# A second queue for the weights of a graph network, and another order for the head of its last layer

## The chip, the cores and the metric

The kernel runs on one core of a Trainium2 chip. The metric is the time of one execution in device microseconds (us), as the median of several runs. A profile of one execution is read beside it. Engines are named as the profile names them: PE (TensorE, with PEld for its weight loads), DVE (VectorE), ACT (ScalarE), POOL (GpSimd) and SP (SyncE). ACT, POOL and SP each issue DMAs on a queue; the letter q behind an engine's name (ACTq) marks that in the trace.

## The reference

There are 16 graphs of 1024 nodes with 128 channels. `x` is [16, 1024, 128], `adj` is [16, 1024, 1024] of zeros and ones. Two layers, each added to its input and normalised over the channels. Cut to what matters:

```python
# layer 0: four steps of a gated graph convolution
h = x
for i in range(4):
    hw = jnp.einsum('bnc,cd->bnd', h, weight[i])
    m = jnp.einsum('bjn,bjd->bnd', adj, hw)
    h = _gru_cell(m, h, w_ih[i], w_hh[i], b_ih[i], b_hh[i])
x = layernorm(x + h * nodemask)
# layer 1: neighbours thinned row by row, then three SAGE steps
adj_d = dilate(adj)                       # each row's removals touch later rows
def sage(x, Wr, Wx, b):
    agg = einsum('bij,bjd->bid', adj_d, x) / clip(sum(adj_d, -1), 1)
    out = agg @ Wr + x @ Wx + b
    return out / max(norm(out), 1e-12) * nodemask
h1 = bn(relu(sage(x, Wr1, Wx1, b1)), g1, be1)   # bn: over all graphs and nodes
h2 = bn(relu(sage(h1, Wr2, Wx2, b2)), g2, be2)
h3 = bn(relu(sage(h2, Wr3, Wx3, b3)), g3, be3)
x = layernorm(x + (concat([h1, h2, h3]) @ Wl + bl) * nodemask)
```

## The kernel before

**Stages.** `Gated` computes layer 0 and, woven into it, `FixPoint` thins the neighbours of layer 1: the GRU's matrix products fill PE, the thinning fills what DVE and ACT have left. Two streams of graphs alternate, so that one's products stand beside the other's element work. `Sage` then makes three passes over all graphs (`first`, `second`, `third`); a batch norm needs the statistics of all 16 graphs before the next pass can begin. `head_weights` makes the last batch norm and what follows from it, and `last`, the head, computes the output.

**Order of the work.** In all these stages the order of the instructions on each engine is the order in which the code emits them (`manual_schedule`), except that some are moved up within their engine where nothing holds them. Each engine runs its instructions one after the other; an instruction that waits holds all that stand behind it on its engine, and DMA issues are such instructions too. Each queue serves its own DMAs.

**Start.** `run` of `Gated` loads x of the first graph (L1021, POOL), then `load_weights` (L947 to L963) issues 14 DMAs on ACT's queue: for each of the four steps 64 KB of `weight`, 192 KB of `w_ih` and 192 KB of `w_hh` (L955, L959; tiles `h_w`, `h_ms`, `h_r`, `h_z`, `h_zh`), then the two biases (L963). POOL's queue brings eight 512 KB tiles of the first graph's adjacency (L1016, `h_a`), as fp32r for the products, and four 256 KB tiles `f_a` for the thinning. `prepare` turns every weight on PE (L974, L977), folds `weight` into `w_ih` (L981) and turns the biases (L986). `begin` (L1049) and the main loop follow: L1092 are the products of the adjacency with the high part (`h_hi`) and the low part (`h_lo`) of h, L1104 the gates.

In a gate, DVE adds (L1116, L1118) and `rest` (L1030) computes the low part for the next step, from a PSUM bank that PE needs again. POOL does the last three operations of the GRU cell (L1123 to L1125).

**h_test.** The kernel for the usual input holds only if the adjacency is zeros and ones. `load_test(n)` (L991 to L994) brings 128 rows of it on SP's queue, `check(n)` (L996) calls `look` (L2028), one DVE pass over the 128x1024 tile. `load_test(0)` is SP's second DMA, its check stands among DVE's operations of the first layer. Any other value sets a flag, and a general version follows, which the input here does not need.

**Third pass.** `third` (L1875 to L1927) goes through 32 units, half graphs, in stages: products of unit i, normalised rows of unit i - 2 (L1429), transposes of unit i - 3 on PE (L1450), ACT's copy of unit i - 4 into `r3` (L1916), statistics of unit i - 5 (L1909). For each unit DVE adds the other product to `acc` (L1927), the sum that the head needs. Its PSUM pool has eight banks: two each of `q_oa` and `s_tr`, two of the double tile `q_ob`.

**Head weights.** `batch_norm(2)` (L1328 to L1333) aggregates the statistics and makes scale and shift, `scaled` (L1336) makes `wr2`, the scaled part of Wl. The shifts of the three batch norms go through Wl into a 48x128 matrix `v`: DVE copies each shift to 48 columns (L1376), PE multiplies (L1377), and a fourth pair (L1379, L1380) brings the bias. `parts` (L1343 to L1350) splits v into three bf16 parts, the rows `r48`.

**Head.** `last` (L1930 to L2001) goes over the graphs. `row(b)` (L1942) takes from r48 what belongs to graph b, on POOL. `head(b)` does two halves: four fp32 products of `r3` with `wr2` (L1953), for the second half a product of `acc` with the unit matrix (L1957), which adds acc in PSUM, and four bf16 products of the mask with the row (L1961). For the first half DVE adds acc instead (L1964). DVE's bn_stats (L1968) and bn_aggr (L1970) make mean and variance of each node, ACT the root (L1972). `norm(b)` on the graph before: DVE makes scale and shift (L1977, L1978), and POOL (L1984, one of eight), ACT (L1988, seven of eight) or, for the last graph, DVE write the normalised result, which a DMA brings out.

## Time and profile before

| | before |
|---|---|
| median of 3 runs | 2176.11 us |
| lowest and highest | 2175.39, 2177.13 us |
| the profiled execution | 2176.16 us |
| its span in the profile | 2174.3 us |
| mean granted clock of PE | 0.988 |
| bytes moved by DMA | 406.16 MB |

The span is the time from the first to the last recorded work; what lies around it belongs to the execution's time too. "Busy" is time with an instruction in work; register, branch and semaphore instructions do not count. In a timeline each line gives start, duration, engine, line of the code, operation, output<-inputs, and how many instructions of a kind stand behind one another (xcount, with their joint duration). In brackets stand the engine's idle time just before and what ended it. Start times overlap a little, because instructions are pipelined. The granted clock tells what share of TensorE's full speed the throttle allowed.

### The profile page before, as it was taken

The numbers are of one execution on the slowest core, as the hardware profiler recorded it, in microseconds if no ns is written. First come the engines' busy times: TensorE is split into PE (matmuls) and PEld (weight loads), VectorE is DVE, ScalarE is ACT, GpSimd is POOL, SyncE is SP. The second block draws the span as 40 slices with busy tenths as digits, with TensorE's granted clock in tenths as the row PEclk, the third lists the DMA queues.
The fourth block names the chain that finished last, engine by engine and source line by source line (L and its number), as shares of the span: only waits on it lengthen the run. The fifth ranks groups of instructions, "written<-read, shape, count | busy, mean of one in ns | idle before, by whom it ended". The sixth has DMA issues, their size and how long they took to land. (4 is left out here: it accounts for less than half of the span.)

```text
span 2174.3 us, 33161 instructions
## 1 busy us (share of the span) xinstructions
PE 2063.3 (95%) x10217; PEld 1438.1 (66%) x10217; DVE 1831.1 (84%) x4313; ACT 1312.8 (60%) x3142; POOL 1324.3 (61%) x1346
## 2 busy tenths in 40 slices
PE   6999999999999999999999978999999889999987
PEld 3666556666556665566655656777777768887876
DVE  4898998988998889998889978888888777676888
ACT  3657557566565656656566466666666545555757
POOL 4458558567467476476575456777777545555852
PEclk9999999999999999999999989999999999999989
DMA  8348356347446276455394349888888677775515
GB/s 258 77 93 252 92 126 225 82 133 214 101 143 195 75 210 155 96 190 132 79 266 104 74 166 318 305 297 307 304 305 306 209 243 271 265 262 185 158 40 157
DMA packets 233856, 406.16 MB, mean 187 GB/s; under 512 B 79042, under 2 KB 100196, under 8 KB 233668
## 3 DMA queue, kind: packets, MB, share of 16 engines
q1 hardware_dynamic: 187844, 284.37, 40.7%
q0 software_dynamic: 41472, 117.46, 20.1%
q10 hardware_dynamic: 4352, 2.11, 0.4%
q8 instruction: 83, 1.36, 0.3%
q14 instruction: 105, 0.86, 0.1%
HBM read 313.48 MB, written 109.25 MB: 194 GB/s over the span
## 5 line engine op out<-in xcount | busy, mean ns | idle before, releaser
L1104 PE MATMUL h_g<-h_h,h_wh 128*128 128x512 f32 x768 | 396.1, 597 | 3.3 <-DVE h_r L1116 3.3
L1104 PE MATMUL h_g<-h_ms,h_wi 128*128 128x512 f32 x768 | 392.3, 592 | 0.0
L1123 POOL TENSOR_TENSOR h_zh<-h_r,h_h 128x512 f32<-128x512 f32 x126 | 174.1, 1382 | 257.9 <-ACT h_r L1119 254.7
L737 DVE TENSOR_TENSOR_SCAN f_rank<-f_a,f_first,f_pd 128x1024 f16<-128x1024 bf16 x128 | 299.4, 2345 | 4.2
L1092 PE MATMUL h_g<-h_a,h_hi 128*128 128x512 f32 x1024 | 278.6, 413 | 1.1 <-DMA h_a<-in_adj_dram 1.0
L1536 POOL CAST p_b<-p_at 128x512 uint8<-128x512 f32 x256 | 219.4, 878 | 84.3 <-DVE p_at L1528 52.3
L1104 PEld LDWEIGHTS h_g<-h_ms,h_wi 128*128 128x128 f32 x768 | 145.6, 190 | 184.2 <-issue 168.6
L1092 PE MATMUL h_g<-h_a,h_lo 128*128 128x512 f32 x1024 | 261.9, 393 | 0.4 <-DVE h_lo L1030 0.4
L1092 PEld LDWEIGHTS h_g<-h_a,h_hi 128*128 128x128 f32 x1024 | 190.1, 188 | 61.7 <-issue 21.0
L1092 PEld LDWEIGHTS h_g<-h_a,h_lo 128*128 128x128 f32 x1024 | 189.8, 188 | 39.0 <-DVE h_lo L1030 0.8
L1104 PEld LDWEIGHTS h_g<-h_h,h_wh 128*128 128x128 f32 x768 | 133.4, 190 | 100.3 <-issue 72.9
L1125 POOL TENSOR_TENSOR h_h<-h_h,h_zh 128x512 f32<-128x512 f32 x126 | 179.9, 1427 | 9.9
L1119 ACT ACTIVATE h_r<-h_r,h_bi 128x512 f32<-128x512 f32 x128 | 92.4, 722 | 150.1 <-DVE h_r L1118 150.1
L1124 POOL TENSOR_TENSOR h_zh<-h_z,h_zh 128x512 f32<-128x512 f32 x126 | 162.0, 1285 | 9.9
L1095 ACT COPY h_ms<-h_g 128x512 f32<-128x512 f32 x128 | 73.8, 576 | 150.7 <-PE h_g L1092 150.7
L1403 ACT ACTIVATE s_junk<-s_o 128x128 bf16<-128x128 f32 x256 | 76.1, 298 | 141.6 <-DVE s_o L1396 141.6
L910 ACT ACTIVATE f_u<-f_rank,f_q 128x128 f16<-128x128 f16 (+7 forms) x128 | 110.6, 867 | 69.7 <-DVE f_rank L850 69.7
L2028 DVE SCALAR_TENSOR_TENSOR p_junk<-p_a 128x1024 bf16<-128x1024 f32 x96 | 125.8, 1311 | 0.0
L1803 PE MATMUL q_ob<-s_wxp,q_xt 128*128 128x256 f32 x512 | 123.5, 385 | 0.0
L778 POOL TENSOR_SCALAR_AFFINE_SELECT f_both<-f_both 128x512 bf16<-128x512 bf16 x32 | 20.4, 639 | 164.2 <-DVE f_both L777 164.2
L1528 DVE SCALAR_TENSOR_TENSOR p_at<-p_nr,p_u 128x128 fp32r<-128x128 bf16 (+1 forms) x192 | 102.4, 543 | 20.2 <-ACT p_at L1520 14.8
L887 ACT ACTIVATE f_pd<-f_rank,f_q 128x128 f32<-128x128 f16 x128 | 59.1, 462 | 96.6 <-DVE f_q L701 93.4
(273 smaller groups left out, 4900.9 us busy)
## 6 DMA issues: line engine op xcount, KB each, us to landing
h_a<-in_adj_dram POOLq DMA_DIRECT2D x128, 512.0 KB, 9.1
p_a<-in_adj_dram SPq DMA_DIRECT2D x96, 512.0 KB
f_a<-in_adj_dram POOLq DMA_DIRECT2D x128, 256.0 KB, 6.5
e_nr<-f_nr SPq DMA_DIRECT2D x128, 256.0 KB
p_nr<-e_nr SPq DMA_DIRECT2D x32, 1024.0 KB
h_test<-in_adj_dram SPq DMA_DIRECT2D x32, 512.0 KB
s_at<-p_b SPq DMA_DIRECT2D x32, 512.0 KB
s_ag<-s_ag SPq DMA_DIRECT2D x64, 256.0 KB
```

The source lines that it names most:

```text
L737: nc.vector.tensor_tensor_scan(out, a, other[:, 0, 0:1].to_broadcast([P, N]), start, op0=ALU.add, op1=ALU.bypass)
L910: nc.scalar.activation(u[:, :n1], rank[:, g, :n1], AF.Abs, bias=q[:, 1, g:g + 1], scale=q[:, 0, g:g + 1])
L1092: nc.tensor.matmul(pm[f], part[:, j, :], st.adj[j][:, half[f]], start=(j == 0 and n == 0), stop=(j == NB - 1 and n == 1))
L1104: nc.tensor.matmul(pg, lhs, rhs, start=(i == 0), stop=(i == len(mm) - 1))
L1119: nc.scalar.activation(r, r, AF.Tanh, bias=bias(self.bi, 2))
L1123: aid.tensor_tensor(d, r, h, ALU.subtract)
L1124: aid.tensor_tensor(d, z, d, ALU.mult)
L1125: aid.tensor_tensor(h, h, d, ALU.add)
L1528: self.nc.vector.scalar_tensor_tensor(g["at"][:, j, c0:c0 + low], v[:, j, c0:c0 + low], 0.0, pu[:, :low], op0=ALU.is_lt, op1=ALU.is_lt)
L1536: self.nc.gpsimd.tensor_copy(g["b", f][:, j, :], g["at"][:, j, f * HF:(f + 1) * HF].bitcast(F32))
L1803: nc.tensor.matmul(pb[:, i], g["xt"][:, f, blk], self.wxp, start=(i % 2 == 0), stop=False)
L2028: nc.vector.scalar_tensor_tensor(junk, a, 0.0, a, op0=ALU.is_gt, op1=ALU.not_equal, accum_out=bad[:, c:c + 1])
```

## The change

- `load_weights`: w_hh's four DMAs and both biases go to SP's queue; `weight` and w_ih stay on ACT's.
- `load_test(0)` goes from SP's queue to POOL's, where it stands behind the second L1125 of the first stream's first layer. DVE's check keeps its place.
- `third` and `last` share one PSUM pool. The head's banks are those of the third pass (`head_banks`); for 8 of the 16 graphs both halves lie in one `q_ob` tile.
- `head_weights` is now within the head's schedule. It first starts the second halves of graphs 0 and 1 with the unit-matrix product (`start_half`), ahead of their other products, then two 128x512 bf16 products into a bank that nobody reads. In PE's order, the two unit products stand between the transposes of the third pass's units 29 and 30, the two idle products behind those of unit 31. After v's products graph 2's half is started too.
- The last unit's addition to `acc` stands on DVE behind the four copies for v. Those for the first two batch norms, which the old order had moved up into earlier passes, now stand with the others; their tile has two buffers as before.
- Row 0 is made by DVE; u_rb has four buffers rather than three.
- The mask products of a half come after the main products of the next half (`half`, `finish`).
- For 15 graphs mean and variance come from six POOL operations on 128x8 tiles (`moments`) in place of eight bn_aggr on DVE; the last graph keeps bn_aggr, behind all its statistics.
- `norm` goes 4 to 7, then 0 to 3, with POOL on two of eight and ACT on six. The root of a graph is emitted after the norm of the graph before.

```diff
--- before.py
+++ after.py
@@ -956,11 +956,11 @@
             for n, src in enumerate((w_ih, w_hh)):
                 t = wk.tile([C, HF], F32, name=next(names))
                 t = self.w_in[l, n] = t[:, :3 * C].rearrange("p (g c) -> p g c", g=3)
-                nc.scalar.dma_start(t, src[l].rearrange("(g p) c -> p g c", p=C))
+                (nc.scalar, nc.sync)[n].dma_start(t, src[l].rearrange("(g p) c -> p g c", p=C))
         t = wk.tile([P, NB, C], F32, name="h_x", bufs=3)
         self.b_in = [t[:L0 * 3, i, :] for i in range(2)]
         for t, src in zip(self.b_in, (b_ih, b_hh)):
-            nc.scalar.dma_start(t, src.rearrange("l (g c) -> (l g) c", c=C))
+            nc.sync.dma_start(t, src.rearrange("l (g c) -> (l g) c", c=C))
 
     def prepare(self):
         nc, ident = self.nc, self.cst["ident"]
@@ -991,7 +991,7 @@
     def load_test(self, n):
         if n < B * 2:
             self.test = self.wk.tile([P, N], F32, name="h_test", bufs=1)
-            self.nc.sync.dma_start(self.test, self.adj[n // 2, n % 2 * P:(n % 2 + 1) * P, :])
+            (self.nc.sync if n else self.nc.gpsimd).dma_start(self.test, self.adj[n // 2, n % 2 * P:(n % 2 + 1) * P, :])
 
     def check(self, n):
         junk = self.wk.tile([P, N], BF, name="h_junk", bufs=1)
@@ -1366,11 +1366,16 @@
         nc.tensor.matmul(v, self.sel01[:, l, :], self.vr, start=(l == 0), stop=True)
         self.parts(v, self.part6, self.r6[:6, :])
 
-    def head_weights(self, ps):
+    def head_weights(self):
         nc, K = self.nc, 3 * B
+        v = self.ps2.tile([P, 4, P], F32, name="s_tr")[:K, 0, :]
+        junk = self.ps2.tile([P, 4, P], F32, name="s_tr").rearrange("p a b -> p (a b)")
+        for b in range(2):
+            self.start_half(b)
+        for i in range(2):
+            nc.tensor.matmul(junk, self.cst["ident_b"], self.mask48[:, :HF], start=True, stop=True)
         self.batch_norm(2)
         self.scaled(self.wr2, self.wl[:, 2, :], 2)
-        v = ps.tile([K, C], F32, name="s_v48")
         for l in range(3):
             beta = self.small.tile([C, K], F32, name="s_beta48")
             nc.vector.tensor_copy(beta, self.ab[l][:, 1:2].to_broadcast([C, K]))
@@ -1378,10 +1383,27 @@
         beta = self.small.tile([C, K], F32, name="s_beta48")
         nc.vector.tensor_copy(beta[:10, :], self.cst["ident"][:10, 9:10].to_broadcast([10, K]))
         nc.tensor.matmul(v, beta[:10, :], self.vr, start=False, stop=True)
+        nc.vector.tensor_add(*self.late)
+        self.start_half(2)
         r48 = self.one.tile([P, C], BF, name="s_r48")
         nc.gpsimd.memset(r48, 0.0)
         self.parts(v, self.part48, r48[:K, :])
         return r48
+
+    def head_banks(self, b):
+        ps = self.ps2
+        if b % 4 in (0, 3):
+            self.banks[b] = [ps.tile([P, 4, C], F32, name="s_tr" if b % 4 else "q_oa") for f in range(2)]
+        else:
+            t = ps.tile([P, 4, 2, C], F32, name="q_ob").rearrange("p a b c -> p (a b) c")
+            self.banks[b] = [t[:, :4, :], t[:, 4:, :]]
+
+    def start_half(self, b):
+
+        acc = self.acc[:, b, 4:, :]
+        self.head_banks(b)
+        self.nc.tensor.matmul(self.banks[b][1].rearrange("p a b -> p (a b)"), self.cst["ident"],
+                              acc.rearrange("p a b -> p (a b)"), start=True, stop=False)
 
 
     def scale_rows(self, b, f, pa, pb, scalar=False):
@@ -1878,7 +1900,7 @@
         with ExitStack() as c:
             pool = lambda name, **k: c.enter_context(tc.tile_pool(name=name, **k))
...
@@ -1924,63 +1946,89 @@
                 if i < len(units):
                     g["ss", f] = self.shared_squares(g["o", f])
                     acc = self.acc[:, b, 4 * f:4 * f + 4, :]
-                    nc.vector.tensor_add(acc, pb[:, :, 1, :], acc)
-
-
-    def last(self, r48):
+                    self.late = acc, pb[:, :, 1, :], acc
+                    if i + 1 < len(units):
+                        nc.vector.tensor_add(*self.late)
+
+
+    def last(self):
         nc, tc, cst = self.nc, self.tc, self.cst
         with ExitStack() as c:
             pool = lambda name, **k: c.enter_context(tc.tile_pool(name=name, **k))
             wk = pool("u_wk", bufs=6)
-            ps = pool("u_ps", bufs=8, space=PSUM)
             c.enter_context(tc.manual_schedule(engines={ET.PE, ET.DVE, ET.Activation, ET.Pool, ET.SP}))
+            r48 = self.head_weights()
             st = {}
 
             def row(b):
                 if b < B:
-                    st["row", b] = wk.tile([P, C], BF, name="u_rb", bufs=3)
-                    nc.gpsimd.tensor_scalar(st["row", b], r48, self.graph[:, b:b + 1], None, op0=ALU.mult)
-
-            def head(b):
-                rb = st.pop(("row", b))
-                row(b + 2)
-                y = wk.tile([P, NB, C], F32, name="u_y")
-                mv = self.small.tile([P, NB, 2], F32, name="p_mv")
-                for f in range(2):
-...
+            def half(b, f):
+
+                ahead = b < 3 and f
+                if f == 0:
+                    row(b + 2)
+                    if b not in self.banks:
+                        self.head_banks(b)
+                pp, acc = self.banks[b][f], self.acc[:, b, 4 * f:4 * f + 4, :]
+                for i in range(4):
+                    nc.tensor.matmul(pp[:, i, :], self.r3[:, b, f, i * P:(i + 1) * P], self.wr2,
+                                     start=(i == 0 and not ahead), stop=False)
+                if f and not ahead:
+                    nc.tensor.matmul(pp.rearrange("p a b -> p (a b)"), cst["ident"],
+                                     acc.rearrange("p a b -> p (a b)"), start=False, stop=False)
+
+            def finish(b, f):
+                pp, acc = self.banks[b][f], self.acc[:, b, 4 * f:4 * f + 4, :]
+                for i in range(4):
+                    k = 4 * f + i
+                    nc.tensor.matmul(pp[:, i, :], self.mask48[:, k * P:(k + 1) * P], st["row", b],
+                                     start=False, stop=(i == 3))
+                if not f:
+                    st["y", b] = wk.tile([P, NB, C], F32, name="u_y")
+                    st["s6", b] = self.small.tile([P, NB, 6], F32, name="u_st")
+                    nc.vector.tensor_add(st["y", b][:, :4, :], pp, acc)
+                s6, src = st["s6", b], pp if f else st["y", b]
+                for i in range(4):
+                    nc.vector.bn_stats(s6[:, 4 * f + i, :], src[:, i, :])
+
+            def moments(b):
+                y, pp, s6 = st.pop(("y", b)), self.banks.pop(b)[1], st.pop(("s6", b))
+                st.pop(("row", b))
+                if b < B - 1:
+
+                    mv = self.small.tile([P, 4, NB], F32, name="u_mv")
+                    total, gap, spread, var = (mv[:, i, :] for i in range(4))
+                    nc.gpsimd.tensor_tensor(gap, s6[:, :, 1], s6[:, :, 4], ALU.subtract)
+                    nc.gpsimd.tensor_tensor(spread, s6[:, :, 2], s6[:, :, 5], ALU.add)
+                    nc.gpsimd.tensor_tensor(gap, gap, gap, ALU.mult)
+                    nc.gpsimd.tensor_scalar(gap, gap, C / 4.0, 0.0, op0=ALU.mult, op1=ALU.add)
+                    nc.gpsimd.tensor_tensor(var, gap, spread, ALU.add)
+                    nc.gpsimd.tensor_tensor(total, s6[:, :, 1], s6[:, :, 4], ALU.add)
+                    st[b] = y, pp, total, var, -0.5, 1.0 / C
+                else:
+                    mv = self.small.tile([P, NB, 2], F32, name="p_mv")
+                    for k in range(NB):
+                        nc.vector.bn_aggr(mv[:, k, :], s6[:, k, :])
+                    st[b] = y, pp, mv[:, :, 0], mv[:, :, 1], -1.0, 1.0
+
+            def root(b):
+                rs = st["rs", b] = self.small.tile([P, 2, NB], F32, name="u_rs")
+                nc.scalar.activation(rs[:, 0, :], st[b][3], AF.Sqrt, bias=self.eps, scale=st[b][5])
 
             def norm(b):
-                y, pp, mv, rs = st.pop(b)
+                y, pp, mean, _, share, _ = st.pop(b)
+                rs = st.pop(("rs", b))
                 nc.vector.reciprocal(rs[:, 0, :], rs[:, 0, :])
-                nc.vector.scalar_tensor_tensor(rs[:, 1, :], mv[:, :, 0], -1.0, rs[:, 0, :],
+                nc.vector.scalar_tensor_tensor(rs[:, 1, :], mean, share, rs[:, 0, :],
                                                op0=ALU.mult, op1=ALU.mult)
-                for k in range(NB):
+                for k in (4, 5, 6, 7, 0, 1, 2, 3):
                     src = pp[:, k - 4, :] if k > 3 else y[:, k, :]
                     scale, shift = rs[:, 0, k:k + 1], rs[:, 1, k:k + 1]
-                    if k == 0 or (b, k) == (B - 1, 1):
+                    if k < 2:
                         nc.gpsimd.tensor_scalar(y[:, k, :], src, scale, shift, op0=ALU.mult, op1=ALU.add)
                     elif b == B - 1 and k > 2:
                         nc.vector.tensor_scalar(y[:, k, :], src, scale, shift, op0=ALU.mult, op1=ALU.add)
@@ -1994,11 +2042,23 @@
 
             row(0)
             row(1)
-            for b in range(B + 1):
-                if b < B:
-                    head(b)
-                if b:
-                    norm(b - 1)
+            halves = [(b, f) for b in range(B) for f in range(2)]
+            for h in range(len(halves) + 1):
+                if h < len(halves):
+                    half(*halves[h])
+                if h < 1:
+                    continue
+                b, f = halves[h - 1]
+                finish(b, f)
+                if f:
+                    moments(b)
+                    if b == B - 1:
+                        root(b)
+                    if b:
+                        norm(b - 1)
+                    if b < B - 1:
+                        root(b)
+            norm(B - 1)
 
     def run(self):
         tc, nc = self.tc, self.nc
@@ -2016,10 +2076,9 @@
         with tc.tile_pool(name="s_psw", bufs=1, space=PSUM) as ps:
             self.weights(2, ps.tile([6, C], F32, name="s_v6"))
         self.r3 = self.ctx.enter_context(tc.tile_pool(name="s_r3p", bufs=1)).tile([C, B, 2, HF], F32, name="s_r3")
-        self.third()
-        with tc.tile_pool(name="s_psw", bufs=1, space=PSUM) as ps:
-            r48 = self.head_weights(ps)
-        self.last(r48)
+        with tc.tile_pool(name="t_ps2", bufs=2, space=PSUM) as self.ps2:
+            self.third()
+            self.last()
 
 
 def look(nc, junk, bad, a, b, k):
```

More of the change, by code (lines that the diff above doesn't have):

```diff
@@ L1880, in third @@
             self.wk = pool("t_wk", bufs=3)
-            self.ps2 = pool("t_ps2", bufs=2, space=PSUM)
+            self.banks = {}
             c.enter_context(tc.manual_schedule(engines={ET.PE, ET.DVE, ET.Activation, ET.Pool, ET.SP}))
@@ L1940, in row @@
                 if b < B:
-                    st["row", b] = wk.tile([P, C], BF, name="u_rb", bufs=3)
-                    nc.gpsimd.tensor_scalar(st["row", b], r48, self.graph[:, b:b + 1], None, op0=ALU.mult)
-            def head(b):
-                rb = st.pop(("row", b))
-                row(b + 2)
-                y = wk.tile([P, NB, C], F32, name="u_y")
-                mv = self.small.tile([P, NB, 2], F32, name="p_mv")
-                for f in range(2):
-                    acc = self.acc[:, b, 4 * f:4 * f + 4, :]
-                    pp = ps.tile([P, 4, C], F32, name="u_p")
-                    for i in range(4):
-                        nc.tensor.matmul(pp[:, i, :], self.r3[:, b, f, i * P:(i + 1) * P], self.wr2,
-                                         start=(i == 0), stop=False)
-                    if f:
-                        nc.tensor.matmul(pp.rearrange("p a b -> p (a b)"), cst["ident"],
-                                         acc.rearrange("p a b -> p (a b)"), start=False, stop=False)
-                    for i in range(4):
-                        k = 4 * f + i
-                        nc.tensor.matmul(pp[:, i, :], self.mask48[:, k * P:(k + 1) * P], rb,
-                                         start=False, stop=(i == 3))
-                    if not f:
-                        nc.vector.tensor_add(y[:, :4, :], pp, acc)
-                    s6 = self.small.tile([P, 4, 6], F32, name="p_st")
-                    src = pp if f else y
-                    for i in range(4):
-                        nc.vector.bn_stats(s6[:, i, :], src[:, i, :])
-                    for i in range(4):
-                        nc.vector.bn_aggr(mv[:, 4 * f + i, :], s6[:, i, :])
-                rs = self.small.tile([P, 2, NB], F32, name="u_rs")
-                nc.scalar.activation(rs[:, 0, :], mv[:, :, 1], AF.Sqrt, bias=self.eps)
-                st[b] = y, pp, mv, rs
@@ new lines, in row @@
+                    st["row", b] = wk.tile([P, C], BF, name="u_rb", bufs=4)
+                    (nc.gpsimd if b else nc.vector).tensor_scalar(st["row", b], r48, self.graph[:, b:b + 1], None,
+                                                                  op0=ALU.mult)
+            def half(b, f):
[11 more added lines that the diff above has]
+                                     acc.rearrange("p a b -> p (a b)"), start=False, stop=False)
```

## The prediction

> **What bounds the kernel now.** The summary and the slices come first: TensorE (PE) is busy for 95% of the span, every other engine for 84% or less, so the time is PE's work plus the places where PE stands still. The slices show two of those, the first and the last.

> ```profile
> span 2174.3 us, 33161 instructions
> PE 2063.3 (95%) x10217; PEld 1438.1 (66%) x10217; DVE 1831.1 (84%) x4313; ACT 1312.8 (60%) x3142; POOL 1324.3 (61%) x1346
> PE   6999999999999999999999978999999889999987
> PEclk9999999999999999999999989999999999999989
> ```

> The change touches exactly these ends, so I read the timeline of each. PE's timeline from 4 to 36 us (start, duration, line, out<-in, count, idle before and its releaser):

> ```profile
> 13.23 0.90 PE L974 MATMUL h_g<-ident,h_r 128*128 128x128 f32 x3 [5.40 <-DMA h_r<-in_L_gnn_w_ih_dram]
> 17.68 0.90 PE L974 MATMUL h_g<-ident,h_r 128*128 128x128 f32 x3 [3.55 <-DMA h_r<-in_L_gnn_w_hh_dram]
> 23.55 0.87 PE L974 MATMUL h_g<-ident,h_z 128*128 128x128 f32 x3 [4.76 <-DMA h_z<-in_L_gnn_w_ih_dram]
> 27.14 0.88 PE L974 MATMUL h_g<-ident,h_z 128*128 128x128 f32 x3 [2.72 <-DMA h_z<-in_L_gnn_w_hh_dram]
> ...
> 33.81 2.09 PE L1092 MATMUL h_g<-h_a,h_hi 128*128 128x512 f32 x8
> ```

> PE waits four times for weights; the last set starts at 28.02, and 5.8 us later the main loop begins (33.81). From there PE has no idle time (26.00 us busy in 34 to 60, 40.00 in 60 to 100): each microsecond by which the loop starts earlier is one off the time, and each stall of PE behind it is one on it.

> The DMA view of 10 to 20 us says why weights are late:

> ```profile
> q0 software_dynamic: 933, 2.75, 90.6%
> q10 hardware_dynamic: 934, 0.45, 22.3%
> ```

> One packet of q0 (POOL's, adjacency) passes for one of q10 (ACT's, weights), 93 a microsecond each, though a weight packet is a sixth as large. From 26 to 27 us, with q0 nearly empty, q10 moves 523.

> **Start: the weights' queue.** Weights' packets number 3824 in all, of which q10 had moved 1259 by 8 us; 2565 are left. With w_hh on SP's queue there would be two weight packets to one of q0. A q0 packet takes 16 x 0.906 / 93.3 = 0.155 us of an engine, a q10 packet 0.038; together 0.193, in which 0.171 passed (16 / 93.4), so a third packet makes the round 0.205 us: 78 packets a microsecond for each queue, 156 for weights.
> From 2 to 5 us q1 (mostly h_test, which leaves) took 77, 78 and 40% of the engines, 1.96 us of all of them, or 1025 weight packets at 523. If none of that is used, 2565 / 156 = 16.4 and the weights end at 24.4; if all is, 1540 / 156 = 9.9 and they end at 17.9. I take the middle, 21.1. With the 5.9 us from the last landing (27.9) to the loop, it starts at 27.0, 6.8 us earlier. The late end gives 30.3, 3.5 earlier. The early end meets another transfer: q0 loses slots (78 rather than 94 a microsecond), so its 1717 packets after 8 us are through at about 27.9; the loop needs its last tile 1.8 us after its begin, so it starts no earlier than 26.1, 7.7 earlier. Gain **6.8** (3.5 to 7.7).
> ACT issues 8 DMAs where it issued 14 (from 3.94 to 23.47 us, two of which stood 6.54 and 4.21 us); SP has nothing else to do then.

> [...]

> **Start: h_test.** SP issues it at 1.24 us; POOL would after its second L1125 of the first layer, which here ends at 58.79. POOL then idles 7.80 us, so the issue delays nothing. Behind it stands DVE's check, in its old place:

> ```profile
> 57.83 2.04 DVE L2028 SCALAR_TENSOR_TENSOR h_junk<-h_test 128x1024 bf16<-128x1024 f32 x1
> ...
> 62.89 0.49 DVE L864 TENSOR_SCALAR f_w<-f_u,f_q 128x1024 bf16<-128x1024 f16 x1 [0.68 <-ACT f_u L913]
> 63.41 0.69 DVE L866 TENSOR_TENSOR f_nr<-f_w,f_a 128x1024 bf16<-128x1024 bf16 x1
> 64.78 0.49 DVE L864 TENSOR_SCALAR f_w<-f_u,f_q 128x1024 bf16<-128x1024 f16 x1 [0.67 <-ACT f_u L913]
> ...
> 66.43 0.74 DVE L1116 SCALAR_TENSOR_TENSOR h_r<-h_g,h_bh,h_r 128x512 f32<-128x512 f32 x1
> 67.28 0.69 DVE L1118 TENSOR_TENSOR h_r<-h_g,h_r 128x512 f32<-128x512 f32 x1
> 67.89 0.68 DVE L1030 TENSOR_TENSOR h_lo<-h_g,h_hi 128x512 fp32r<-128x512 f32 x1
> ```

> Such a 512 KB load lands after 3.4 us (e_sum, when DMA is quiet) to 5.5 (the fastest h_a; h_x takes 5.1): 4.6 taken, so the check starts at 63.4, 5.6 late. The waits for ACT (0.68 + 0.67) cover 1.35; beside an idle POOL the check takes about 0.8 less (1.22 at 96.12). L1030 is then 3.4 late, and PE, whose product at 68.82 needs its bank and has 0.25 spare, stands 3.2 us (2.0 to 4.2). This moves with the loop, so it counts in full. Cost **3.2**; net of the start -3.6 (-7.7 + 2.0 = -5.7, to -3.5 + 4.2 = +0.7).

> **Head: before its first products.** PE's timeline between third pass and head:

> ```profile
> 2099.81 1.09 PE L1450 MATMUL s_tr<-ident,s_r 128*128 128x128 f32 x4 [1.25 <-DVE s_r L1429]
> 2101.57 1.09 PE L1377 MATMUL s_v<-s_wl,s_beta 128*48 128x128 f32 x4 [0.67 <-ACT s_r L1916]
> 2104.82 0.66 PE L1377 MATMUL s_v<-s_wl,s_beta 128*48 128x128 f32 x2 [2.17 <-DVE s_beta L1376]
> 2105.41 0.66 PE L1380 MATMUL s_v<-s_vr,s_beta 10*48 10x128 f32 x2
> 2106.85 0.55 PE L1953 MATMUL u_p<-s_wr,s_r 128*128 128x128 f32 x1 [0.78 <-DVE s_rest L1344]
> ```

> DVE's chain sets it: L1429, bn_stats, L1328, root, wr2 (ends 2104.41), beta, v, split, row(0) on POOL (2108.43, 0.60), masks 2109.09. In order:
> - L1927 (0.68) goes behind v: some 0.5 off the last two normalisations, 1.25 of PE's wait being for them.
> - The betas 0 and 1, copied in earlier passes until now, follow wr2 on DVE, and the tile has two buffers, so beta 2 waits for PE: four copies (0.19) and products (0.33 warm, twice that cold), two more than now, +0.7 warm, +1.0 cold; I take +0.8.
> - row(0) on DVE takes 0.34 (L1350, the nearest) less a hand-over: -0.5 of 0.60 + 0.1.
> - Three unit products of 0.86 leave the head's PE stretch for idle time ahead: -2.6. The first two stand between the transposes of units 29 and 30; 1.7 us in PE's gaps of 0.40 and 1.25 push those transposes by up to 0.6, already in DVE's slack at 2099.6 if the clock is full.
> - Clock: PE is granted 1.00 until 2099.4 and 0.50 until 2113.04. 6.2 us of products there cost 3.1 over the warm rows (1.09 against 0.63 for four transposes, 2.04 against 1.11 for L1953). Products in the gaps could keep it (-3.1) or not (0).

> These do not add in full. DVE's chain to the first masks gains 0.5 - 0.8 + 0.5 = 0.2. Behind the first masks PE is the bound, without idle time until the end: there the three unit products are missing (-2.6), and of the clock's 3.1 I count half (-1.5, between all and nothing). The transposes pushed back cost +0.5. PE's end: -0.2 - 2.6 - 1.5 + 0.5 = **-3.8** (-1 to -6).

> [...]

> **Head: steady state.** PE's period per graph is 3.20 us without idle (0.86 + 0.23 + 0.95 + 0.22 + 0.95; 2118.57 to 2121.78). DVE's is the same (0.72, 0.79, 0.32, 0.81, 0.28, 0.28); moving bn_aggr (0.60) to POOL frees DVE, not PE: 0. ACT loses one of seven (0.38), hidden too. The wait that is new: both halves of 8 graphs share one tile, so masks of half 1 wait for DVE's addition of half 0; a half behind, they have over a microsecond for its 0.7. I estimate 0.1 each: **+0.8** (0 to 2).
> POOL: row 0.60, two norms 0.88, six 128x8 operations. Their bounds are 0.106 (memset 128x16) and 0.44 (128x128); nearest is 48x3, 0.182, so 0.15 plus a gap of 0.08: 1.48 + 6 x 0.23 = 2.9, under 3.20.
> Behind PE's end: now DVE does bn_stats and aggr of half 1; then the addition, eight bn_aggr (0.6) and masks come later in order: **+1.3** (0.5 to 2). Head: -3.8 + 0.8 + 1.3 = **-1.7** (+1 to -4).

> **Sum.** Profiled run 2176.16 (span 2174.3 and 1.86 around it; the median 2176.11 is 0.05 less): 2176.16 - 3.6 - 1.7 = **2170.9**; ends 2176.16 - 5.7 - 4 = 2166.5 and 2176.16 + 0.7 + 1 = 2177.9.

> **Rivals.**
> - A: the sum, 2166.5 to 2171.7: 0.55.
> - B: weights move no faster, or h_test's wait eats it: for it speaks DMA at 9 tenths until 27 us, against it the small share (22%) of weights. Start 0, head -1.7: 2174.5. 0.18.
> - C: the clock is already low when the unit products run (2 x 1.71 us in front of two transposes), so they delay the chain by 2: start -3.6, head about 0: 2172.6. 0.12.
> - D, slower: POOL becomes the head's bound. At 0.29 us a moment operation POOL's graph takes 3.20; from there it decides. At 0.44 it takes 1.48 + 2.64 = 4.1, 0.9 more on 15 graphs, +14: 2170.9 + 14 = 2185. 0.15.

> [...]

> Measurement tells 0.2% (4.35 us) from no change. Faster than 2171.8 is A: 0.55; same (B and C): 0.30; slower (D): 0.15. Range **2166.5 to 2178**: all but D and a rest of A.

> **What would show it.** L974's last wait ends near 21 us, L1092 starts near 27; the check waits about 5.6 us for h_test and PE about 3 for L1030; granted clock 1.00 through the head; PE's period 3.20 with POOL's moments under 0.2 each; POOL as releaser of ACT's roots would be D. I am wrong if weights and adjacency end together as now, or if the head's chain waits on POOL.

## The result and the profile after

The changed kernel is faster by 0.4%: 2165.86 us (median of 5 runs, 2164.98 to 2169.4) beside 2176.7 for the kernel before (5 runs), ratio 0.9958 with a 95% interval of 0.9946 to 0.9969, so 6.7 to 11.8 us. Run once more beside other kernels it gave 0.9963 (0.9949 to 0.9976), so 8.1 us. The forecast was 2170.9, 5.3 us less than the profiled run before; the gain by the medians, 10.8, is twice that. By the ratio the time is 2167.0 beside 2176.16, near the fast end of the range (2166.5), and the median itself lies 0.6 past that end. The profiled run after took 2169.40, the slowest of its five and 6.8 less than before's 2176.16; its span is 7.0 shorter.

The page after, the lines that answer to those of before:

```profile
span 2167.3 us, 33169 instructions
PE 2065.3 (95%) x10218; PEld 1441.3 (67%) x10219; DVE 1826.0 (84%) x4194; ACT 1307.0 (60%) x3127; POOL 1345.7 (62%) x1451
PE   7999999999999999999999979999999989999987
PEclk9999999999999999999999989999999999999999
```

The shares say nothing here: the same 95%, of a shorter span. The ends have to be read one by one. PE's timeline at the start, after:

```profile
...
9.79 1.54 PE L974 MATMUL h_g<-ident,h_r 128*128 128x128 f32 x6 [2.82 <-DMA h_r<-in_L_gnn_w_ih_dram]
...
16.59 1.51 PE L974 MATMUL h_g<-ident,h_z 128*128 128x128 f32 x6 [5.05 <-DMA h_z<-in_L_gnn_w_ih_dram]
...
22.20 1.52 PE L974 MATMUL h_g<-ident,h_zh 128*128 128x128 f32 x6 [3.88 <-DMA h_zh<-in_L_gnn_w_ih_dram]
...
23.72 4.29 PE L981 MATMUL h_g<-h_wi,h_w 128*128 128x384 f32 x8
...
28.84 2.09 PE L1092 MATMUL h_g<-h_a,h_hi 128*128 128x512 f32 x8
```

The last weights are there at 22.2 rather than 28.0, the loop begins at 28.84 rather than 33.81: 4.97 earlier. Between the two lie 6.64 us, where before had 5.79; L981 alone takes 4.29 where it took 3.46. DMA's view of 10 to 20 us, and of 12 to 14 within it, after:

```profile
q0 software_dynamic: 880, 2.51, 85.2%
q10 hardware_dynamic: 806, 0.39, 15.5%
q1 hardware_dynamic: 546, 0.25, 12.7%
```

```profile
q0 software_dynamic: 163, 0.30, 79.5%
q1 hardware_dynamic: 163, 0.08, 19.5%
q10 hardware_dynamic: 164, 0.08, 13.3%
```

From 12 to 14 us all three have work and each moves 82 packets a microsecond (78 forecast). SP's share is through by 18 us, ACT's, the longer one, by 22. DVE's and PE's timelines around h_test's check, after:

```profile
57.66 1.23 DVE L2087 SCALAR_TENSOR_TENSOR h_junk<-h_test 128x1024 bf16<-128x1024 f32 x1 [4.71 <-DMA h_test<-in_adj_dram]
...
63.83 0.75 DVE L1116 SCALAR_TENSOR_TENSOR h_r<-h_g,h_bh,h_r 128x512 f32<-128x512 f32 x1
64.68 0.69 DVE L1118 TENSOR_TENSOR h_r<-h_g,h_r 128x512 f32<-128x512 f32 x1
65.29 0.68 DVE L1030 TENSOR_TENSOR h_lo<-h_g,h_hi 128x512 fp32r<-128x512 f32 x1
```

```profile
64.64 1.13 PE L1104 MATMUL h_g<-h_h,h_wh 128*128 128x512 f32 x2 [0.61 <-DVE h_r L1116]
```

DVE does wait for h_test, 4.71 us, and L1116 comes 2.37 late measured from the loop's begin. But PE loses 0.61 there. The same product of PE before, which waits for nothing:

```profile
68.82 1.02 PE L1104 MATMUL h_g<-h_h,h_wh 128*128 128x512 f32 x2
```

And the head, PE's timeline after:

```profile
2091.28 1.31 PE L1405 MATMUL q_oa<-s_acc,ident 128*128 128x512 f32 x2
2092.39 1.91 PE L1405 MATMUL q_ob<-s_acc,ident 128*128 128x512 f32 x2
2094.09 1.63 PE L1472 MATMUL s_tr<-ident,s_r 128*128 128x128 f32 x8
2095.83 0.38 PE L1376 MATMUL s_tr<-s_mask,ident_b 128*128 128x512 bf16 x1
2099.70 1.57 PE L1382 MATMUL s_tr<-s_wl,s_beta 128*48 128x128 f32 x6 [3.50 <-DVE s_beta L1381]
2101.20 0.66 PE L1385 MATMUL s_tr<-s_vr,s_beta 10*48 10x128 f32 x2
2101.78 2.08 PE L1405 MATMUL q_ob<-s_acc,ident 128*128 128x512 f32 x2
2103.65 2.85 PE L1978 MATMUL q_oa<-s_wr,s_r 128*128 128x128 f32 x16
2106.34 0.39 PE L1988 MATMUL q_oa<-u_rb,s_mask 128*128 128x128 bf16 x4
```

From v's products on PE stands still only once more until its last, for 0.18 us (2112.53, waiting for DVE's addition of a graph whose two halves share a tile), so the wait of 3.50 us ahead of them is the last one that counts. The unit product of graph 2 (2101.78) lies behind it, in the stretch that PE bounds, and at half clock (0.50 below). The granted clock by stretches (columns: window, length, busy time of PE, PEld, DVE, ACT, POOL, clock, DMA share, GB/s), after:

```profile
2091.90:2095.30 3.40, 3.40 (x9) 1.78 (x9) 2.62 (x7) 0.28 (x2) 0.00 (x0) 0.50 0.00 0
2095.30:2098.70 3.40, 0.80 (x5) 0.34 (x4) 2.47 (x4) 1.34 (x3) 0.00 (x0) 1.00 0.00 0
2098.70:2105.50 6.80, 5.80 (x19) 3.78 (x20) 4.22 (x18) 0.00 (x0) 0.93 (x2) 0.50 0.00 0
```

The clock falls at 2091.9, recovers at 2095.3, and falls again at 2098.7, late in PE's wait before v, until 2105.5: one length of 3.4 and then two. POOL's moments, after, one graph:

```profile
2149.53 0.21 POOL L2005 TENSOR_TENSOR u_mv<-u_st 128x8 f32<-128x8 f32 x1 [1.07 <-DVE u_rs L2025]
2149.70 0.20 POOL L2006 TENSOR_TENSOR u_mv<-u_st 128x8 f32<-128x8 f32 x1
2149.86 0.20 POOL L2007 TENSOR_TENSOR u_mv<-u_mv 128x8 f32<-128x8 f32 x1
2150.15 0.20 POOL L2008 TENSOR_SCALAR u_mv<-u_mv 128x8 f32<-128x8 f32 x1
...
2150.79 0.88 POOL L2032 TENSOR_SCALAR u_y<-u_y,u_rs 128x128 f32<-128x128 f32 x2
```

At most 0.21 each, 1.26 for six: POOL's graph takes 0.60 + 0.88 + 1.26 = 2.74, under PE's 3.20.

**By sections.** One execution of a kernel differs from the next by several microseconds (after's five runs take 2164.98 to 2169.4), so I cut each profile at five events: the loop's first product; the PE product that waits for L1116 at 243.16 in before; DVE's last product sum of the third pass (L1396, 2094.73 in before); PE's last product; the span's end.

| profile | loop begins | to 243.16's event | to third's last sum | to PE's end | to the end | span |
|---|---|---|---|---|---|---|
| before | 33.81 | 209.35 | 1851.57 | 66.71 | 12.86 | 2174.3 |
| after | 28.84 | 210.07 | 1850.21 | 64.46 | 13.72 | 2167.3 |
| after again (e13) | 30.00 | 210.13 | 1850.64 | 64.48 | 13.35 | 2168.6 |
| e1 start only | 28.91 | 209.95 | 1851.42 | 66.54 | 12.58 | 2169.4 |
| e2 head only | 33.88 | 208.95 | 1853.36 | 62.31 | 13.40 | 2171.9 |
| e3 test early | 29.17 | 210.05 | 1849.43 | 64.45 | 14.00 | 2167.1 |
| e4 more idle | 29.37 | 209.93 | 1850.90 | 64.15 | 13.35 | 2167.7 |
| e5 aggr on DVE | 27.02 | 210.35 | 1850.06 | 65.51 | 13.66 | 2166.6 |
| e6 none ahead | 28.65 | 210.60 | 1848.95 | 65.53 | 13.87 | 2167.6 |
| e7 beta ahead | 26.96 | 210.34 | 1849.78 | 61.68 | 14.14 | 2162.9 |
| e9 moments twice | 26.71 | 210.22 | 1849.77 | 72.47 | 14.63 | 2173.8 |
| e10 late in place | 27.82 | 210.18 | 1850.12 | 64.70 | 13.38 | 2166.2 |
| e11 early, beta | 28.07 | 210.09 | 1849.81 | 61.67 | 13.36 | 2163.0 |
| e12 as e11, idle | 31.39 | 209.14 | 1851.50 | 61.69 | 13.88 | 2167.6 |

After against before: -4.97 + 0.72 - 1.36 - 2.25 + 0.86 = -7.0. The third term lies in stages that the change leaves alone, but for two small copies that only before and e1 have there. Those 1850 us spread over 4.4 us in the table (1848.95 to 1853.36). The clock is one thing that differs in them. PE's timeline of before and then of after, at the third pass's begin:

```profile
1986.86 3.54 PE L1803 MATMUL q_ob<-s_wxp,q_xt 128*128 128x256 f32 x8
...
1991.41 1.89 PE L1803 MATMUL q_ob<-s_wxp,q_xt 128*128 128x256 f32 x8
```

```profile
1982.37 1.89 PE L1825 MATMUL q_ob<-s_wxp,q_xt 128*128 128x256 f32 x8
```

Eight products take 3.54 in one and 1.89 in the other: before was granted half clock there (0.50 from 1986.78 to 1990.19), after full (1.00). But this place does not explain the term. The whole stretch, before and then after (columns as above):

```profile
243.16:2094.73 1851.57, 1783.65 (x8947) 1254.99 (x8947) 1578.65 (x3569) 1134.46 (x2767) 1167.92 (x1159) 0.99 0.63 193
238.91:2089.12 1850.21, 1785.18 (x8947) 1257.37 (x8947) 1580.35 (x3566) 1134.59 (x2767) 1166.98 (x1160) 0.99 0.63 193
```

PE is busy 1.53 us longer after, and idle 2.89 less (65.03 rather than 67.92). By the traces' clock records half clock adds up to 27.3 us there before and to 37.6 after, so on the whole the clock was against the changed kernel. Why PE stood still less is open.

### The profile page after: what moved, and what is told of

The parts are those of the page before. It is cut to its first block, busy times and chain, and to the rows that moved or that the text cites. A ratio compares the mean times of both kernels' runs of the same rounds, so it can differ in the third digit from the quotient of the medians.

```text
span 2167.3 us, 33169 instructions
## 1 busy us (share of the span) xinstructions
PE 2065.3 (95%) x10218; PEld 1441.3 (67%) x10219; DVE 1826.0 (84%) x4194; ACT 1307.0 (60%) x3127; POOL 1345.7 (62%) x1451
## 3 DMA queue, kind: packets, MB, share of 16 engines
q8 instruction: 83, 1.36, 0.3%
q10 hardware_dynamic: 2704, 1.31, 0.2%
## 5 line engine op out<-in xcount | busy, mean ns | idle before, releaser
L1123 POOL TENSOR_TENSOR h_zh<-h_r,h_h 128x512 f32<-128x512 f32 x126 | 174.3, 1383 | 256.9 <-ACT h_r L1119 253.7
L1092 PE MATMUL h_g<-h_a,h_hi 128*128 128x512 f32 x1024 | 278.0, 413 | 0.2
L1092 PE MATMUL h_g<-h_a,h_lo 128*128 128x512 f32 x1024 | 262.1, 393 | 0.3 <-DVE h_lo L1030 0.3
L1092 PEld LDWEIGHTS h_g<-h_a,h_hi 128*128 128x128 f32 x1024 | 190.1, 188 | 60.0 <-issue 21.5
L1092 PEld LDWEIGHTS h_g<-h_a,h_lo 128*128 128x128 f32 x1024 | 189.7, 188 | 39.3 <-DVE h_lo L1030 1.2
L1125 POOL TENSOR_TENSOR h_h<-h_h,h_zh 128x512 f32<-128x512 f32 x126 | 179.9, 1428 | 9.9
```

The lines of the kernel that those rows point to most:

```text
L1092: nc.tensor.matmul(pm[f], part[:, j, :], st.adj[j][:, half[f]], start=(j == 0 and n == 0), stop=(j == NB - 1 and n == 1))
L1123: aid.tensor_tensor(d, r, h, ALU.subtract)
L1125: aid.tensor_tensor(h, h, d, ALU.add)
```

## The experiments

Theory: the start and the head each gain about what their edits take off PE's path, and the rest is the clock's phase, that is, where its half-clock stretches fall; the two rows above do not bear out that last part. Rivals: a shift alone gains more by its phase; POOL or DVE bounds the head; the order of the copies for v, the products ahead and the late addition each have another size than the prediction gave them.

**e1 and e2: each half alone.** e1 is the kernel before with the edits of `load_weights` and `load_test`; e2 is the changed kernel with these taken back.

> The kernel before with the two edits at the start alone (w_hh and biases on SP's queue, h_test on POOL's). Theory from the two traces: the loop starts 5.0 us earlier, PE then waits about 0.7 us for DVE's late L1116, so -4.2 us against before, and every later stage is shifted by that. The prediction's sizes (6.8 earlier, stall 3.2) give -3.6. Rival, the clock: the shift alone also moves the later stages against the half-clock stretches; then the time falls by 5.5 to 6.5 us, and the third pass begins without the half clock that before's trace has at 1985 to 1990 us. Rival B of the prediction (no gain at the start): 0.

> The changed kernel with the start as before (all weights on ACT's queue, h_test on SP's). If the start is worth 4.2 us and the head has the rest of the medians' difference, -6 to -6.5 us against before. If the head is worth what the prediction gave it, -1.7. If 1.7 to 2 us of the difference come from the clock's phase in the third pass, -4.

e1: 2169.75 us, ratio 0.9974 (0.9965 to 0.9983), -5.7 (3.7 to 7.6). e2: 2173.74, ratio 0.9994 (0.9984 to 1.0003), -1.3 (-3.5 to +0.7). e1's time alone fits the theory and the rival on the phase. Its profile speaks for the theory: 4.90 - 0.60 = 4.3 gained up to the second event, and the third pass begins at half clock as in before (its first eight products take 3.25, at full clock 1.89), so the shift did not remove that. What is left, 0.6, is spread over the other three sections. e2's time is that of its second case (-1.7), but its profile is not: the head gains 4.40 to PE's end, of which it gives back 0.54, so 3.86; 1.79 is lost in the unchanged stages, which have no half clock at the third pass's begin here (its first eight products take 1.89), and yet are the longest of the table. The head had full clock there during the first two unit products (1.02 each, in the changed kernel 1.31 and 1.91), and behind v the first 16 main products take 2.43, in the changed kernel 2.85: with the same code in the head, e2's is 2.15 shorter to PE's end. The two halves add to -7.0 by their times, as in the profiled run; why the changed kernel's medians give 8.1 and 10.8 no run shows.

**e3: h_test issued before POOL's first L1123.**

```diff
-            if n == 9 and s == 0:
+            if n == 9 and s == 0 and (b0 or l):
                 self.load_test(b0 // 2 * L0 + l)
+            if n == 5 and s == 0 and b0 == 0 and l == 0:
+                self.load_test(0)
```

> The changed kernel with h_test issued on POOL's queue before the first L1123 rather than behind the second L1125. Theory: the load lands before DVE's check, L1116 is on time, and PE's one wait of 0.61 us at the first stream's gates goes: 0.7 us faster than the changed kernel. The prediction's size of that stall would make it 3.2 us faster. Rival: the earlier transfer delays the next loads of adjacency and PE waits for them instead: no gain.

2168.3 us, ratio 0.9961 (0.9947 to 0.9974): within its interval the same as the changed kernel. PE's waits from 28 to 250 us in e3, and then in the changed kernel from 29 to 250 (columns: total, times, longest):

```profile
PE f_pd L902 <- DVE f_x L894: 1.9, 1, 1.9
PE h_g L1037 <- ACT h_r L1113: 0.6, 1, 0.6
PE h_g L1104 <- DVE h_r L1116: 0.3, 1, 0.3
```

```profile
PE h_g L1104 <- DVE h_r L1116: 0.9, 2, 0.6
PE h_g L1037 <- ACT h_r L1113: 0.8, 1, 0.8
PE h_g L1092 <- DVE h_lo L1030: 0.3, 1, 0.3
PE f_pd L902 <- DVE f_x L894: 0.3, 1, 0.3
```

The wait of 0.6 goes, as the theory has it: in the nine profiles with the late h_test it is 0.60 to 0.78, in e3, e11 and e12 it is not there. A wait of 1.9 comes at 198 us, for an operation of DVE (L894). It came in e11 too, and not in e12, which has the same edit. A DMA transposition that DVE waits for at 179 us is not shown to be behind it: that wait is 2.94 in e3 and 2.43 in e11, but 2.34 in e10 too, where PE has no such wait. So the 0.6 can be given back later; whether by chance or by cause stays open.

**e4: 12 idle products rather than 2** (`range(2)` becomes `range(12)`).

> The changed kernel with 12 idle products rather than 2 behind the transposes of unit 31. Theory: what is left of the half clock in the head (2099 to 2105.5 us in the profile) comes from PE's 3.5 us without work before v's products; with products there the clock stays full, and the run is 1 to 2 us faster than the changed kernel where that kernel lost the clock, and the runs lie closer together. Rival: the clock does not answer to so few products, and ten more of 0.22 to 0.43 us delay v's: 0 to +1.5 us.

2169.15 us, ratio 0.9962 (0.9948 to 0.9975): the same. The head to PE's end takes 64.15, 0.31 less, and PE's wait before v is 1.12 rather than 3.50. Ten more products did not hold the clock: v's products ran at full clock (1.09 and 0.41, in after 1.57 and 0.66), the 16 behind them mostly not (3.27 us, in e7 at full clock 1.95).

**e5: bn_aggr on DVE for every graph** (`if b < B - 1` becomes `if b < 0`).

> The changed kernel with eight bn_aggr on DVE for every graph and no moments on POOL. Theory: PE is the bound of the head at 3.20 us a graph with either, and DVE with bn_aggr needs 3.20 too, so the time from the third pass's last DVE step to PE's end stays within 0.5 us of the changed kernel's 64.46. Rival: DVE, now as long as PE and started a half later, becomes the bound: 0.1 to 0.2 a graph, 2 to 3 us longer.

2168.64 us, ratio 0.9971 (0.9962 to 0.998). PE's end comes 1.05 later. PE's timeline says where:

```profile
2108.77 0.38 PE L1988 MATMUL q_ob<-u_rb,s_mask 128*128 128x128 bf16 x4 [0.32 <-DVE u_y L1993]
...
2111.90 0.38 PE L1988 MATMUL q_ob<-u_rb,s_mask 128*128 128x128 bf16 x4 [0.63 <-DVE u_y L1993]
```

That is the new wait on the shared `q_ob` tile, 0.95 in all, until PE and DVE run at the same 3.20. With the moments on POOL it comes once, 0.18 us (2112.53 above), and PE waits for nothing from 2114 to its end. So this wait accounts for 0.77 of the 1.05.

**e6: no products ahead, no idle ones.**

```diff
-        for b in range(2):
-            self.start_half(b)
-        for i in range(2):
-            nc.tensor.matmul(junk, self.cst["ident_b"], self.mask48[:, :HF], start=True, stop=True)
...
-        self.start_half(2)
...
-                ahead = b < 3 and f
+                ahead = False
```

> The changed kernel without the three unit-matrix products ahead and without the two idle products; graphs 0 to 2 have theirs in place as the others. Theory: three products of 0.86 us come back into PE's bound stretch and leave idle time, so the time from the third pass's last DVE step to PE's end grows by 2.1 (2.6 less the 0.5 by which they push the transposes). If the clock answers to them, up to 2 us more. Rival C of the prediction (they delay the chain by 2): no change or faster.

2169.52 us, ratio 0.9971 (0.9962 to 0.998). PE's end comes 1.07 later, half of what was expected, with products at half clock, by what they take, from the last four transposes (1.09 at 2092.90, 0.61 at full clock) through the first 16 main products (3.78, 1.95 at full), where after has 3.41 us at full clock in between. The last batch norm's aggregation comes 0.84 sooner (7.17 rather than 8.01 after the third pass's last sum): so much the products in front of the transposes cost, being at half clock (1.31 and 1.91). In e2 and e9, where they had full clock (1.02 each), it stands at 6.78 and 6.79. Rival C's mechanism is real, its size here 0.84 and not 2.

**e7: copies and products for v ahead of the last batch norm.**

```diff
+        def shift(l):
+            beta = self.small.tile([C, K], F32, name=f"s_beta48_{l}", bufs=1)
+            nc.vector.tensor_copy(beta, self.ab[l][:, 1:2].to_broadcast([C, K]))
+            nc.tensor.matmul(v, beta, self.wl[:, l, :], start=(l == 0), stop=(l == 2))
+        for l in range(2):
+            shift(l)
+        beta = self.small.tile([C, K], F32, name="s_beta48_3", bufs=1)
+        nc.vector.tensor_copy(beta[:10, :], self.cst["ident"][:10, 9:10].to_broadcast([10, K]))
+        nc.tensor.matmul(v, beta[:10, :], self.vr, start=False, stop=False)
         self.batch_norm(2)
         self.scaled(self.wr2, self.wl[:, 2, :], 2)
+        shift(2)
```

(The loop over l and the bias behind `scaled` go.)

> The changed kernel with each shift's 48 columns in a tile of its own, and the products for v of the first two shifts and of the bias emitted ahead of the last batch norm. Theory: the order of these copies costs the chain to v what the prediction said (0.8) or more; here v's split begins 1.3 us sooner after wr2, and PE's end comes 0.8 to 1.5 us sooner after the third pass's last DVE step. Rival: the 0.67 us addition that stands behind the copies is then on the chain: gain 0.5 or less.

2167.74 us, ratio 0.9964 (0.9952 to 0.9976), and its profile is the shortest span, 2162.9. PE's end comes 2.78 sooner after the third pass. PE's timeline:

```profile
2095.05 0.64 PE L1380 MATMUL s_tr<-s_wl,s_beta 128*48 128x128 f32 x4 [0.27 <-PE s_tr L1476]
2095.61 0.41 PE L1386 MATMUL s_tr<-s_vr,s_beta 10*48 10x128 f32 x2
2098.18 0.42 PE L1380 MATMUL s_tr<-s_wl,s_beta 128*48 128x128 f32 x2 [2.15 <-DVE s_beta L1379]
2098.78 1.13 PE L1409 MATMUL q_ob<-s_acc,ident 128*128 128x512 f32 x2 [0.18 <-DVE s_acc L1390]
2099.74 1.95 PE L1982 MATMUL q_oa<-s_wr,s_r 128*128 128x128 f32 x16
```

That is more than the 0.8 to 1.5 that was expected. The wait before v ends as late as in the changed kernel (2.48 after the aggregation's begin, there 2.57). But behind it v's products hold PE for 0.60 (2098.18 to 2098.78, a wait of 0.18 included) and not 2.08 (2099.70 to 2101.78): 1.5 from the order, though the 2.08 were at half clock too. The clock, full here from 2093.6 on (1.00 from 2095 to 2106, where after has 0.50 from 2098.7 to 2105.5), gives 1.8: the unit product holds PE for 0.96, not 1.87, and from the first of the 16 products to PE's end it takes 49.02, not 49.93. And 0.6 is lost ahead of the aggregation, which comes 8.62 after the third pass's last sum, not 8.01.

**e9: the moments made twice** (the six operations in a loop over `range(2)`; the last result is used).

> The changed kernel with each graph's six POOL operations made twice (the first result is not used). It tests rival D's point. POOL's graph: 0.60 + 0.88 + 12 x 0.21 = 4.0 us, PE's 3.20. Theory: past 3.20 POOL sets the pace, 0.8 on 15 graphs less what the buffers hold back, 9 to 12 us slower than the changed kernel. Rival: POOL's result is needed late enough (buffers of several graphs), so less than 3 us slower.

2178.14 us, ratio 1.0013 (1.0004 to 1.0022), so some 11 us slower than the changed kernel's 0.9963; in the profile PE's end comes 8.0 later, less than the 9 to 12 expected. ACT's timeline names POOL as the releaser, graph after graph:

```profile
2139.14 0.30 ACT L2021 ACTIVATE u_rs<-u_mv,s_eps 128x8 f32<-128x8 f32 x1 [0.56 <-POOL u_mv L2010]
...
2143.06 0.30 ACT L2021 ACTIVATE u_rs<-u_mv,s_eps 128x8 f32<-128x8 f32 x1 [0.55 <-POOL u_mv L2010]
```

3.92 us a graph, the 4.0 of the sum. So rival D's mechanism is real: at 3.92, past PE's 3.20, POOL sets the pace. By the sums the changed kernel's 2.74 is 0.46 a graph on the safe side; that the pace turns at 3.20 itself was not tried.

**e10: the late addition in its old place** (`tensor_add(*self.late)` for every unit in `third`, none in the head).

> The changed kernel with the last unit's addition to acc back in the third pass, ahead of the last two normalisations on DVE. Theory: its 0.68 us is on DVE's chain to the last batch norm, so that chain (the third pass's last DVE step to the aggregation, 8.01 in the changed kernel's profile) grows by 0.5 to 0.7; but behind v's copies it also held the chain there, so PE's end moves by 0 to +0.5. The prediction gave the move 0.5. Rival: the chain waits for the transposes that the unit products push back, and the move is worth nothing.

2168.25 us, ratio 0.9966 (0.9952 to 0.9979). The aggregation comes 0.46 later, PE's end 0.24: the move is worth a quarter of a microsecond.

**e11, e12, e13: both mends, with more idle products, and the changed kernel again.** e11 has the edits of e3 and e7, e12 also ten idle products.

> The changed kernel with h_test issued early (as in e3) and the shifts' copies and products ahead of the last batch norm (as in e7). Theory: both add up, 0.6 and 1.6 us (and up to 1.2 where the clock stays full), so 2 to 3.5 us faster than the changed kernel run beside it, and the fastest of all. Rival: what h_test's early load frees is given back at a wait for a DMA transposition, so only e7's part is seen.

> As e11, with ten idle products rather than two. If the clock answers to products in PE's gap before v, the head runs at full clock from there and it is up to 1 us faster than e11; if not (as e4, whose head gained 0.3 us), within 0.5 us of e11.

> The changed kernel itself once more, beside the other three on the same chip, for its spread and a second profile. The e-runs share its start edit, and their loop starts between 26.7 and 29.4 us by their profiles; if that is a spread of the start and not of those edits, this one lies in the same range, and the time is 2164 to 2169 us.

e11 2165.98 (0.9951, 0.9938 to 0.9965), e12 2166.75 (0.9948, 0.9934 to 0.9962), e13 2168.93 (0.9963, 0.9949 to 0.9976). e11 has the lowest median of the four kernels that ran beside each other; the intervals overlap. By sections its head is e7's (61.67), and so is e12's (61.69): with v in order the idle products add nothing. e13's loop begins at 30.00, outside the 26.7 to 29.4 that was expected, and e12's at 31.39: the begin lies between 26.7 and 31.4 in twelve profiles with one and the same queue edit, so that spread is of the start itself.

The later place of the mask products, the new order of the norm and row 0 on DVE were not tried alone.

## Why the prediction was right, step by step

The sign was right, and so was the start's mechanism. The two halves came out near their forecasts in the profiled run: start -3.6 forecast, -4.25 measured; head -1.7 forecast, -1.39 measured (-2.25 + 0.86). That is partly luck: in each half, terms that were too large stand against each other. The remaining 1.36 of the profile lies in stages that the change leaves alone, and so, at least in part, must the rest of the medians' 10.8; no run accounts for it.

- **Weights.** The packet sum held (82 for 78 a microsecond; last weights at 22.2 for 21.1). The gain is 4.97, not 6.8: 1.1 of the difference is that landing, 0.74 the stretch from there to the loop, 5.9 taken and 6.64 measured, nearly all of it in L981. In the twelve profiles with this edit the loop begins 2.4 to 7.1 earlier than in before, 5.2 on average, so 4.97 is one draw of many. The feared meeting with `h_a` did not show. (ACT's 14 issues in before begin at 0.79, not at 3.94, and three of them stood over 4 us, 6.54, 4.21 and 4.28; nothing in the sum hangs on it.)
- **h_test: the step that failed** is "PE, whose product at 68.82 needs its bank and has 0.25 spare", the bank being L1030's. In after the product starts at 64.64, before L1030 does (65.29); it waits for L1116, which in before ends at 67.17 and has 1.65 spare. With L1116 late by 2.37 (3.4 was the forecast for DVE; the load took 3.9, not 4.6) that leaves 0.72, not 3.2. The two errors, 1.8 too much gain and 2.5 too much cost, nearly cancelled, by luck.
- **The head's path.** The prediction let DVE's chain to the first masks set PE's end. In after the first masks (2106.34) wait for nothing, and their row is ready 1.7 earlier (2104.62): PE bounds already from v's products on. So the 0.8 for v's order and the 0.5 for row(0) are not on the path as priced, though both happened: from the aggregation's begin to v's split it is 4.76 against 3.83, and from L1350's end to the row's end 0.38 against 0.93. Without graph 2's unit product, the first of the head's main products (L1978, L1953 before) comes 4.65 after the aggregation's begin, before 4.57. What v's order costs PE is another thing, its products in the bound stretch, and e7 shows what is to be had there.
- **Products ahead.** -2.6 forecast, +0.5 for the transposes. In before the three unit products took 1.71 (at half clock), 0.86 and 0.86 of PE's bound stretch. Two went into idle time; graph 2's stands behind v's products on the bound path and takes 1.87 there, at half clock: 1.6 net. With the idle ones, e6 makes the three worth 1.07 after the 0.84 that they cost.
- **Late addition.** 0.5 on the chain: 0.46, of which 0.24 reach PE's end. With the 0.84 of the unit products that makes the aggregation 0.4 later than in before; it is 0.46 (8.01 against 7.55 after the third pass's last sum).
- **The clock.** From the first of the main products on, 6.2 us were at half clock before (2106.85 to 2113.04), 1.9 after (2103.65 to 2105.53). Without the unit products that gives some 1.2, 1.5 forecast. But v's products and graph 2's unit product, which now stand in the bound stretch, ran at half clock too (2099.70 to 2103.65), and granted clock 1.00 through the head did not come. e2, with fewer products at half clock, is 2.15 better.
- **The sum to PE's end.** Aggregation +0.5, graph 2's unit product in front +1.9, three unit products out of the rest -3.4, the clock there -1.2: -2.2, the -2.25 of the table.
- **The shared tile and the moments.** +0.8 and 0 forecast; it is one wait of 0.18, and e5 shows that the one buys the other: with bn_aggr on DVE PE's end comes 1.05 later, 0.77 of it by that very wait.
- **POOL.** 0.23 an operation forecast, 0.21 measured, where DVE's operations on 128x8 tiles (L2025, L2026) take 0.17 to 0.19; D did not come, and e9 shows that POOL does set the pace when its graph takes 3.92.
- **Tail.** +1.3 forecast, +0.86 (+0.49 in e13).

## What to carry to other kernels

Price a late operation by the product that waits for its own buffer: a bank's name and its spare must be followed in the trace, not taken from the last instruction of the chain. Work moved "into idle time" counts only where it stands ahead of the wait that ends last; behind it, it is on the path. Where two executions of unchanged code differ by more than the change, cut the profiles at common events and compare sections.
